# Moving tap transforms, loads and last products in a graph layer on Trainium2

## The chip, the cores and the metric

The kernel runs on one core of one Trainium2 chip. The metric is the device time of one execution in microseconds. The engines are named as the profile names them: PE (TensorE, matmuls), PEld (its weight loads), DVE (VectorE), ACT (ScalarE), POOL (GpSimd) and SP (SyncE, which here only issues transfers). DMAs are issued from the queues of SP, ACT and POOL.

## The reference, cut to what matters

x has 32 batches of 512 tokens by 256 channels, adj is 32 x 512 x 512. All is float32.

```python
h = jnp.maximum(_layernorm(x, axis=-1), 0.0)
out = x + gnn(h, adj)

def gnn(x, mask):
    xc = jnp.transpose(x, (0, 2, 1))
    c = relu(bn1(conv1d(xc, conv1_w, 0)))            # kernel size 1
    c = bn2(conv1d(c, conv2_w, 8))                   # kernel size 17
    x_conv = jnp.transpose(relu(c + xc), (0, 2, 1))
    s = x @ w_se.T + b_se                            # 3 features
    A = jnp.exp(-squared_distance(s, s)) * mask
    x_nmp = A @ relu(x @ w_msg.T + b_msg)
    gi = concat([x_conv, x_nmp]) @ w_ih.T + b_ih     # r, z, n
    gh = x @ w_hh.T + b_hh                           # r, z, n
    r = sigmoid(gi_r + gh_r); z = sigmoid(gi_z + gh_z)
    n = tanh(gi_n + r * gh_n)
    return (1.0 - z) * n + z * x
```

## The kernel before

The long convolution is done in the frequency domain. A window of 64 tokens is transformed with 80 points, so a batch has 8 windows and 16 batches make a group of 128 windows; there are two groups. The 80 rows of a spectrum are 40 units of two.

**Weights to frequencies.** The 17 taps of conv2 are loaded in eight pieces (`load_taps`, L239; tile w2p, two buffers, which the unscaled w1 of conv1 also uses once). A piece takes five DMAs, four of 16 taps and one for the seventeenth of all four quarters. `weights_to_freq` (L246) makes one step: four products `pw` with the `taps` matrix, copied out by ACT and DVE into `wst`; a piece has four steps. Each pair of steps fills an SI group of four, which four SP DMAs store to `wd` (L269). In the first step of a group DVE copies two of the four results and ACT two, in the second DVE copies one and ACT three.

**First part, once per group** (`first_part`, L779). For each batch b: `statistics` (DVE, and POOL for the power), `normalise` (DVE, tile xn), `transpose_h` (PE phT, DVE hT, store hd), `conv1` (PE pc, DVE and ACT h), `windows_to_freq` (PE px, ACT xf). The statistics run two batches ahead of conv1. In group one the 32 tap steps are spread over the batches by `between(b)`, at first two per batch, in batches 7 and 14 three; it also issues the remaining weight loads on SP. Before the first layer norm of group one, bn1's scale and shift are spread over rows by `bn1_row` (L183: ACT diagonals, PE row) and w1 is scaled by them.

**Nodes, once per group** (`nodes`, L880). Per batch: `message`, `features`, `factors`, `affinity`, `aggregate` (PE pm, psl, psr, pd, pn), and between them the products of spectra unit by unit (`product`, L367: PE py, ACT and DVE y), which `prepare` (L356) readies on POOL (wsum, both). Of group one, three units are left over; they are worked off in group two's first part by `fill()`, from the list `left`.

**Late part.** The gates of pairs of batches, with seven products where a plain 2 x 2 block scheme has eight (`gates_rz`, `gate_n`); POOL makes the operand sums. The last pair has its z gate after n (`last_z`, L637), so that the output can be blended, transposed, added to x and stored piece by piece.

**What sets the order.** Both first parts and the late part stand in `tc.manual_schedule()`: each engine runs their instructions in the order in which the code writes them. `nodes` is not in it; there the framework orders the instructions, also where its end meets the first part of group two. PSUM has eight banks of 128 x 512, handed out by `bank`.

The lines that issue the loads at the start and at group two:

```python
            load_w1()
            load_x(0)
            load_x(1)
            load_taps(gen, 0, nc.sync)
...
                combine = combine_weights()
...
                for b in range(GB, GB + 3):
                    load_x(b, nc.gpsimd)
```

Of the kernel before, what the change touches and what calls it, by code (L numbers as in the profile page):

```python
# [15 lines left out]
P = 128  # L16
# [49 lines left out]
def gnn_layer(  # L66
# [38 lines left out]
    def bank(name):  # L105
        return psum.tile([P, N], FP, tag="bank", name=name)
# [20 lines left out]
    ncol = vecs.shape[1]  # L127
    vec = consts.tile([P, ncol], FP, name="vec")
    nc.scalar.dma_start(vec, vecs)
    w1 = early.tile([P, DC, D], FP, name="w1")  # L130
    fwd = early.tile([P, 2 * L], FP, name="fwd")
    nc.scalar.dma_start(fwd, nc.inline_tensor(fwd_np, name="dft_fwd").ap())
    taps = early.tile([P, ROWS], FP, name="taps")
    nc.scalar.dma_start(taps, nc.inline_tensor(taps_np, name="dft_taps").ap())
    back = consts.tile([P, back_np.shape[1]], FP, name="back")

    GC = G // P
# [51 lines left out]
    def load_w1():  # L189

        t = W2P["w1"] = pools["gen"].tile([P, PI, D], FP, tag="w2p", name="w1_in", bufs=2)
        load_rows(t[:, :DC], w1T, nc.scalar)

    def scale_w1():
        t = W2P.pop("w1")
# [39 lines left out]
    PI = 8  # L235
    SI = 4
    W2P, WST, STATS = {}, {}, {}

    def load_taps(gen, pc, queue=nc.gpsimd):  # L239
        t = W2P[pc] = gen.tile([P, PI, D], FP, tag="w2p", name=f"w2p_{pc}", bufs=2)  # L240
        src = w2T.rearrange("(q i) k o -> q k i o", q=4)[:, :, PI * pc : PI * (pc + 1)]
        for q in range(4):
            queue.dma_start(t[32 * q : 32 * q + 16], src[q, 0:16])
        queue.dma_start(t[16::32], src[:, 16])

    def weights_to_freq(gen, pc, i):  # L246

# [389 lines left out]
    def last_z(p, terms):  # L637

        d, o, ks = RZ[p], 1, range(K3)

        def blended(src, other, i, j, t=slice(0, N)):
            z, dst = d[:, DC + i, j, t], d[:, i, j, t]
            if other is not None:
                nc.vector.tensor_add(z, other[:, t], src[:, t])
                src = z
            g = DC + i
            nc.scalar.activation(z, src, AF.Sigmoid, bias=brz[:, g : g + 1], scale=1.0)
            nc.vector.tensor_mul(dst, dst, z)
            js, half = slice(t.start // 32, t.stop // 32), slice(32 * i, 32 * (i + 1))
            if (p, j) not in OUT:  # L650
                OUT[p, j] = pools["late"].tile([P, N // 32, D // 4], FP, tag="o", name=f"o_{p}_{j}", bufs=2)
            nc.vector.transpose(OUT[p, j][:, js, half], dst.rearrange("p (j k) -> p j k", k=32))
            x = XP[p][j][:, js, half]
            nc.vector.tensor_add(x, x, OUT[p, j][:, js, half])

        b1, b2, b3, b4 = (bank(f"pz{k}_{p}") for k in range(1, 5))
        into(b1, Q1, o, ks, terms, True)
        p1 = temp("p1", f"z{p}")
        nc.scalar.copy(p1, b1)
        into(b2, Q6, o, ks, terms, True)  # L660
        u2 = temp("u2", f"z{p}")
        nc.vector.tensor_add(u2, p1, b2)
        into(b1, Q2, o, ks, terms, False)
        blended(b1, None, 0, 0)
        early_out(p, 1, 1)
        into(b2, Q7, o, ks, terms, False)
        u3 = temp("u3", f"z{p}")
        nc.vector.tensor_add(u3, p1, b2)
        early_out(p, 0, 1)
        into(b4, Q4, o, ks, terms, True)  # L670
        blended(b4, u3, 1, 0)
        store(p, 0, [nc.sync, nc.scalar])
        into(b3, Q5, o, ks, terms, True)
        blended(b3, u3, 1, 1)
        for h in range(2):
            t = slice(h * N // 2, (h + 1) * N // 2)
            into(b3, Q3, o, ks, terms, False, t)
            blended(b3, u2, 0, 1, t)
            store(p, 1, [nc.sync, nc.scalar], t)

    def gate_n(p, terms, last):
# [50 lines left out]
        closing(x3[1], 0, 1)  # L732
        for i, j in ((0, 0), (1, 1), (1, 0), (0, 1)):

            nc.vector.tensor_sub(rz[:, i, j, :], HP[p][:, 2 * i + j, :], nt[:, i, j, :])
            if last and j == 0:
                early_out(p, i, j)
            elif not last:

                blend(p, i, j, nc.gpsimd if p == B // 2 - 2 and i != j else nc.vector)  # L740


    def early_out(p, i, j):
        if (i, j) == (0, 0):
            OUT[p] = pools["work"].tile([P, N // 32, D // 4], FP, tag="x", name=f"on_{p}", bufs=3)
        OUT[p, j] = OUT[p]
        to_tokens(p, j, i)
        o = OUT.pop((p, j))
        if i != j:
            nc.vector.tensor_add(XP[p][j], XP[p][j], o)  # L750

    def blend(p, i, j, engine):
        n, d = NT[p][:, i, j, :], RZ[p][:, i, j, :]
# [25 lines left out]
    def first_part(g, freq, between, left=()):  # L779
# [6 lines left out]
        if g == 0:  # L786
            t = XN[b0] = pools["first"].tile([P, NC, D], FP, tag="xn", name="rows", bufs=2)
            ones, diags = t[:, 0, :P], t[:, 1:3, :].rearrange("p i (c m) -> p i c m", m=P)
            nc.vector.memset(ones, 1.0)
            batch_norm("bn1", scale1, shift1, nc.gpsimd)  # L790
            bn1_row(0, scale1, ones, diags)
            bn1_row(1, shift1, ones, diags)
        statistics(b0)
        normalise(b0)
        if g == 0:
# [8 lines left out]
        fill()  # L804
        statistics(b0 + 1)
        transpose_h(b0)
        normalise(b0 + 1)
        fill()
        for b in range(b0, b1):
            if b + 3 < b1:  # L810
                load_x(b + 3, nc.gpsimd)
            if b == b0:
                if g == 0:
                    for steps in between(0):
                        for step in steps:
                            step()
                conv1(b)
                fill()
            if b + 2 < b1:
# [32 lines left out]
    with tc.tile_pool(name="freq", bufs=1) as fpool:  # L852
# [3 lines left out]
        with phase("first", "gen"):  # L856
            gen = pools["gen"]
            per = N // D
            steps = [partial(weights_to_freq, gen, pc, i) for pc in range(QI // PI) for i in range(0, PI, per)]
            load_w1()  # L860
            load_x(0)
            load_x(1)
            load_taps(gen, 0, nc.sync)

            def between(b):
                if b % 2 == 0 and b // 2 + 1 < QI // PI:
                    load_taps(gen, b // 2 + 1)
                if 1 <= b <= len(load_weights):
                    load_weights[b - 1]()

                mine = spread(steps, b, GB - 1) if b < GB - 1 else [partial(load_unit, 0, u) for u in range(3)]
                return mine[:1], mine[1:]

            with tc.manual_schedule():
                xf = first_part(0, freq_tile, between)
# [41 lines left out]
        with phase("pw"):  # L917
            with phase("nodes"):
                nodes(0, xf, range(UNITS - LEFT), GB)
            with phase("first", "sums"):  # L920
                combine = combine_weights()

                def between(b):
# [4 lines left out]
                    two = [partial(sum_unit, pools["pw"], 1, b - GB + 3)] if b > GB - 3 else []  # L928
                    return combine[b - 2] if 1 < b < len(combine) + 2 else [], two

                for b in range(GB, GB + 3):
                    load_x(b, nc.gpsimd)

                pw, (u0, u1, u2) = pools["pw"], range(UNITS - LEFT, UNITS)
                left = [[partial(prepare, pw, 0, u1, xf), partial(product, pw, 0, u0, xf)],
                        [partial(prepare, pw, 0, u2, xf)],
                        [partial(product, pw, 0, u1, xf)],
                        [partial(product, pw, 0, u2, xf)]]
# [83 lines left out]
```

## Time and profile before

| | us |
|---|---|
| median of 5 runs | 1865.26 |
| lowest and highest | 1861.1, 1869.67 |
| the profiled execution | 1868.94 |
| its span, first to last instruction | 1867.2 |
| PE, DVE, ACT, POOL busy in it | 1828.3, 1115.0, 578.0, 579.1 |

A page row gives the line of the kernel, the engine, the operation, output<-inputs, shapes and count, then busy time, the mean of one, and the idle time of the engine just before with what ended it. A timeline row begins with start and length in us. A row of a window table gives the window, its length, and busy times with counts in brackets for PE, PEld, DVE, ACT and POOL, then the granted PE clock as a share of full speed, the DMA engines' busy share and GB/s.

### The profile page before, as it was taken

To read this page: it belongs to the slowest core of one execution; us is meant where nothing else is said; L and a number is where in the kernel's file an instruction comes from. 1 tells how busy PE (TensorE), PEld (TensorE's weight loads), DVE (VectorE), ACT (ScalarE), POOL (GpSimd) and SP (SyncE) were. 2 spreads that over 40 slices of the span, in tenths; PEclk is the share of its full clock that TensorE was granted. 3 is DMA by queue.
4 is the path that set the end of the run, shared out by engine and by line. 5 is a ranking of instruction groups with operands and counts; after the bars stand their busy time and mean duration, and the time that the engine had idled before them with its cause. 6 is when DMAs were issued, how large, how long until landed. Compare 5 with 4: busy or idle time off the path is not lost.

```text
span 1867.2 us, 20076 instructions
## 1 busy us (share of the span) xinstructions
PE 1828.3 (98%) x6598; PEld 1090.1 (58%) x6598; DVE 1115.0 (60%) x2238; ACT 578.0 (31%) x1075; POOL 579.1 (31%) x563
## 2 busy tenths in 40 slices
PE   7999999999899999999999999999999999999997
PEld 5777666666798666666555544555455544555443
DVE  6775655564796565555165566645665466645666
ACT  3455434332145343333222212222122221222121
POOL 3321234334332343442613322132212322133220
PEclk8999999999899999999999999999999999999999
DMA  7998988865467988767613442244422442234412
GB/s 208 301 267 234 227 238 234 226 176 187 174 224 219 222 254 239 230 190 238 179 47 72 119 118 85 38 114 119 112 69 56 118 119 87 53 97 118 118 28 41
DMA packets 306299, 289.25 MB, mean 155 GB/s; under 512 B 148028, under 2 KB 235612, under 8 KB 305812
## 3 DMA queue, kind: packets, MB, share of 16 engines
q1 hardware_dynamic: 279716, 222.64, 44.8%
q10 hardware_dynamic: 19024, 38.68, 5.9%
q0 software_dynamic: 7456, 26.65, 5.1%
q8 instruction: 53, 0.87, 0.2%
q14 instruction: 50, 0.41, 0.1%
HBM read 191.50 MB, written 96.40 MB: 154 GB/s over the span
## 4 chain that ended last, share of the span: by engine, by line
PE 89%; DMA 3%; issue 3%; DVE 2%; POOL 2%; ACT 1%; SPq 0%; ACTq 0%; POOLq 0%; DVEq 0%
PE pg L585 28%; PE pn L585 14%; PE py L385 10%; PE pn L480 10%; PE pc L320 6%; PE pm L431 5%; PE pc L573 5%; PE px L335 3%; PE pw L256 2%; PE pd L466 2%; PE phT L307 1%; DMA hT<-hd 1%; DMA sw<-ws 1%; PE psr L455 1%; PE pz L585 0%
## 5 line engine op out<-in xcount | busy, mean ns | idle before, releaser
L480 PE MATMUL pn<-A,msg 128*128 128x512 f32 x512 | 225.0, 593 | 0.0
L585 PE MATMUL pg<-hp,sw 128*128 128x512 f32 x434 | 221.8, 593 | 0.7 <-DVE rz L604 0.5
L585 PE MATMUL pg<-cp,sw 128*128 128x512 f32 x434 | 221.7, 592 | 0.3 <-DMA sw<-ws 0.3
L585 PE MATMUL pg<-np,sw 128*128 128x512 f32 x434 | 221.6, 592 | 0.0
L563 POOL TENSOR_TENSOR hp<-hp 128x512 f32<-128x512 f32 x64 | 80.4, 1266 | 412.8 <-DMA hp<-hd 351.7
L364 POOL TENSOR_TENSOR both<-xf 128x256 f32<-128x256 f32 x78 | 60.6, 777 | 333.2 <-PE py L385 299.4
L480 PEld LDWEIGHTS pn<-A,msg 128*128 128x128 f32 x512 | 97.1, 190 | 110.6 <-issue 107.7
L385 PE MATMUL py<-wt,both 128*128 128x256 f32 x624 | 150.4, 384 | 0.7 <-issue 0.7
L563 POOL TENSOR_TENSOR cp<-cp 128x512 f32<-128x512 f32 x64 | 80.4, 1268 | 225.8 <-ACT cp L579 224.5
L600 ACT ACTIVATE rz<-rz,brz 128x512 f32<-128x512 f32 x93 | 67.0, 721 | 260.2 <-DVE rz L604 260.2
L392 DVE TENSOR_TENSOR y<-y,py 128x256 f32<-128x256 f32 x78 | 31.8, 408 | 192.7 <-ACT y L391 192.7
L585 PEld LDWEIGHTS pg<-hp,sw 128*128 128x128 f32 x434 | 82.2, 190 | 104.7 <-issue 97.6
L585 PEld LDWEIGHTS pg<-cp,sw 128*128 128x128 f32 x434 | 82.4, 190 | 104.5 <-issue 103.3
L585 PEld LDWEIGHTS pg<-np,sw 128*128 128x128 f32 x434 | 82.5, 190 | 103.8 <-issue 103.8
L385 PEld LDWEIGHTS py<-wt,both 128*128 128x128 f32 x624 | 114.2, 190 | 43.3 <-issue 28.0
L472 DVE TENSOR_TENSOR A<-e,at 128x512 f32<-128x512 f32 x128 | 112.5, 916 | 36.3 <-ACT e L469 36.0
L320 PE MATMUL pc<-w,hT 128*128 128x256 f32 x512 | 124.6, 400 | 1.9 <-DVE hT L308 1.9
L351 POOL TENSOR_TENSOR wsum<-wt 128x512 f32<-128x512 f32 x78 | 107.9, 1384 | 44.5 <-DMA wt<-wd 41.4
L431 PE MATMUL pm<-wmsg,hq 128*128 128x259 f32 x512 | 117.9, 382 | 1.6 <-ACT hq L417 1.0
L704 ACT ACTIVATE nt<-nt,vech 128x512 f32<-128x512 f32 x64 | 46.2, 722 | 233.9 <-DVE nt L703 233.9
L585 PE MATMUL pn<-np,sw 128*128 128x512 f32 x224 | 114.4, 592 | 0.0
L585 PE MATMUL pn<-hp,sw 128*128 128x512 f32 x224 | 114.4, 592 | 0.0
(138 smaller groups left out, 2956.8 us busy)
## 6 DMA issues: line engine op xcount, KB each, us to landing
wt<-wd SPq DMA_DIRECT2D x160, 256.0 KB, 3.8
adj<-in_adj_dram SPq DMA_DIRECT2D x128, 256.0 KB, 5.6
wd<-wst SPq DMA_DIRECT2D x64, 320.0 KB, 5.1
yd<-y ACTq DMA_DIRECT2D x80, 256.0 KB, 3.5
yt<-yd SPq DMA_DIRECT2D x30, 640.0 KB, 7.5
hd<-hT SPq DMA_DIRECT2D x32, 512.0 KB, 4.8
nd<-nmp ACTq DMA_DIRECT2D x32, 512.0 KB, 3.7
xb<-in_x_dram SPq DMA_DIRECT2D x128, 128.0 KB, 3.7
```

Source lines behind the costliest of these rows:

```text
L320: nc.tensor.matmul(p[:, j, :], HT[b][:, ic, c * P : (c + 1) * P], w1[:, ic, :], start=(ic == 0), stop=(ic == DC - 1))
L335: nc.tensor.matmul(p[:, j * 2 * L : (j + 1) * 2 * L], H1[b][:, c0 + j, ic * P : (ic + 1) * P], fwd, start=True, stop=True)
L351: nc.gpsimd.tensor_tensor(t, WT[g, u][:, 0], WT[g, u][:, 1], op=ALU.add)
L364: nc.gpsimd.tensor_tensor(both[:, 0], re, im, op=ALU.add)
L385: nc.tensor.matmul(dst, v[:, ic, :], w[:, ic, :], start=(ic == 0), stop=(ic == DC - 1))
L431: nc.tensor.matmul(p[:, : D + NS], hq[:, ic, c * P : (c + 1) * P], wmsg[:, ic, :], start=(ic == 0), stop=(ic == DC - 1))
L472: nc.vector.tensor_mul(A[b][:, mc, :], e, at)
L480: nc.tensor.matmul(p, MSG[b][:, mc, dc * P : (dc + 1) * P], A[b][:, mc, :], start=(mc == 0), stop=(mc == NC - 1))
L563: nc.gpsimd.tensor_tensor(t[:, dst, :], t[:, a, :], t[:, b, :], op=sub)
L573: nc.tensor.matmul(bk[:, t0:t1], YT[p][j][:, c, oc * P : (oc + 1) * P], back[:, n : n + t1 - t0], start=(c == 0), stop=(c == len(spans) - ...
L585: nc.tensor.matmul(bk[:, t], sw[:, k, q, o, :], terms[k][q][:, t], start=(first and i == 0), stop=(i == len(ks) - 1), skip_group_check=True)
L600: nc.scalar.activation(rz[:, g, j, :], src, AF.Sigmoid, bias=brz[:, g : g + 1], scale=1.0)
```

## The change

Four things, of which the words name three.

- Start: the taps matrix and the first tap piece are loaded ahead of w1, x of batch 1 and fwd; the piece by SP and ACT, w1 by POOL. Of the piece's four steps, the first runs before the bn1 rows, the second between them and the statistics of batch 0, the third and fourth ahead of conv1 of batch 0. The other 28 steps go two to each of batches 1 to 14; each later piece is loaded one batch before its first step.
- Group two: its first three x are loaded by SP, ahead of the gate weights, instead of by POOL. The first left-over product follows the transposes of the group's first batch; before, it preceded them.
- Last gate: the last product of z (Q3) goes in halves to two banks of its own instead of adding to bank b3; VectorE adds b3 to u2 for it.
- Last pair: the four subtractions and one of the two additions to x run on POOL instead of DVE.

```diff
+    taps = early.tile([P, ROWS], FP, name="taps")
+    nc.scalar.dma_start(taps, nc.inline_tensor(taps_np, name="dft_taps").ap())
     w1 = early.tile([P, DC, D], FP, name="w1")
     fwd = early.tile([P, 2 * L], FP, name="fwd")
-    nc.scalar.dma_start(fwd, nc.inline_tensor(fwd_np, name="dft_fwd").ap())
-    taps = early.tile([P, ROWS], FP, name="taps")
-    nc.scalar.dma_start(taps, nc.inline_tensor(taps_np, name="dft_taps").ap())
...
-        load_rows(t[:, :DC], w1T, nc.scalar)
+        load_rows(t[:, :DC], w1T, nc.gpsimd)
...
-    def load_taps(gen, pc, queue=nc.gpsimd):
+    def load_taps(gen, pc, queues):
...
-            queue.dma_start(t[32 * q : 32 * q + 16], src[q, 0:16])
-        queue.dma_start(t[16::32], src[:, 16])
+            queues[q % len(queues)].dma_start(t[32 * q : 32 * q + 16], src[q, 0:16])
+        queues[-1].dma_start(t[16::32], src[:, 16])
...
-        b1, b2, b3, b4 = (bank(f"pz{k}_{p}") for k in range(1, 5))
+        b1, b2, b3, b4, *b5 = (bank(f"pz{k}_{p}") for k in range(1, 7))
...
         into(b3, Q5, o, ks, terms, True)
         blended(b3, u3, 1, 1)
+        nc.vector.tensor_add(u2, u2, b3)
         for h in range(2):
             t = slice(h * N // 2, (h + 1) * N // 2)
-            into(b3, Q3, o, ks, terms, False, t)
-            blended(b3, u2, 0, 1, t)
+            into(b5[h], Q3, o, ks, terms, True, t)
+            blended(b5[h], u2, 0, 1, t)
             store(p, 1, [nc.sync, nc.scalar], t)
...
-            nc.vector.tensor_sub(rz[:, i, j, :], HP[p][:, 2 * i + j, :], nt[:, i, j, :])
+            (nc.gpsimd if last else nc.vector).tensor_tensor(rz[:, i, j, :], HP[p][:, 2 * i + j, :], nt[:, i, j, :],
+                                                             op=ALU.subtract)
...
-            nc.vector.tensor_add(XP[p][j], XP[p][j], o)
+            (nc.gpsimd if j else nc.vector).tensor_tensor(XP[p][j], XP[p][j], o, op=ALU.add)
...
             batch_norm("bn1", scale1, shift1, nc.gpsimd)
+            one, two = between(0)
+            one[0]()
             bn1_row(0, scale1, ones, diags)
             bn1_row(1, shift1, ones, diags)
+            one[1]()
         statistics(b0)
         normalise(b0)
...
         statistics(b0 + 1)
         transpose_h(b0)
+        fill()
         normalise(b0 + 1)
         fill()
...
                 if g == 0:
-                    for steps in between(0):
-                        for step in steps:
-                            step()
+                    for step in two:
+                        step()
                 conv1(b)
                 fill()
...
+            load_x(0)
+            load_taps(gen, 0, [nc.sync, nc.scalar])
             load_w1()
-            load_x(0)
             load_x(1)
-            load_taps(gen, 0, nc.sync)
+            nc.scalar.dma_start(fwd, nc.inline_tensor(fwd_np, name="dft_fwd").ap())
+            first, rest = steps[: PI // per], steps[PI // per :]
 
             def between(b):
+                if b == 0:
+                    return first[:2], [partial(load_taps, gen, 1, [nc.gpsimd])] + first[2:]
                 if b % 2 == 0 and b // 2 + 1 < QI // PI:
-                    load_taps(gen, b // 2 + 1)
+                    load_taps(gen, b // 2 + 1, [nc.gpsimd])
...
-                mine = spread(steps, b, GB - 1) if b < GB - 1 else [partial(load_unit, 0, u) for u in range(3)]
+                mine = spread(rest, b - 1, GB - 2) if b < GB - 1 else [partial(load_unit, 0, u) for u in range(3)]
...
+                for b in range(GB, GB + 3):
+                    load_x(b)
                 combine = combine_weights()
...
-                for b in range(GB, GB + 3):
-                    load_x(b, nc.gpsimd)
...
-                left = [[partial(prepare, pw, 0, u1, xf), partial(product, pw, 0, u0, xf)],
+                left = [[partial(prepare, pw, 0, u1, xf)],
+                        [partial(product, pw, 0, u0, xf)],
                         [partial(prepare, pw, 0, u2, xf)],
```

## The prediction

> **What bounds the kernel now.** I read the page's share and slice rows first, then stages of the span one by one, then the timelines of the three places that the diff touches.
>
> ```profile
> span 1867.2 us, 20076 instructions
> PE   7999999999899999999999999999999999999997
> PEclk8999999999899999999999999999999999999999
> ...
> PE 89%; DMA 3%; issue 3%; DVE 2%; POOL 2%; ACT 1%; SPq 0%; ACTq 0%; POOLq 0%; DVEq 0%
> ```
>
> TensorE (PE) is full nearly everywhere; only the first, the eleventh and the last slice are not. The busy times by stage (columns: length, then PE, weight load, DVE, ACT, POOL, clock, DMA) say how much is open:
>
> ```profile
> 0.00:20.00 20.00, 10.55 (x39) 7.07 (x40) 11.18 (x38) 5.54 (x11) 7.98 (x20) 0.88 0.75 180
> 455.00:500.00 45.00, 37.98 (x140) 27.98 (x139) 25.31 (x71) 5.25 (x11) 19.29 (x22) 0.85 0.57 193
> 1780.00:1868.00 88.00, 76.13 (x186) 34.60 (x184) 59.33 (x88) 16.54 (x26) 11.31 (x8) 0.96 0.18 36
> ```
>
> PE idles 9.5 us, 7 us and 12 us there, and loses more to a half clock. The change can only win or lose in these places and in what they shift. The timeline of the start:
>
> ```profile
> 5.46 1.40 DVE L284 BATCH_NORM_STATS2 stats<-x 128x6 f32<-128x256 f32 x4 [3.71 <-DMA x<-in_x_dram]
> 9.42 1.92 PE L307 MATMUL phT<-ident,xn 128*128 128x128 f32 x8
> 13.23 3.71 PE L256 MATMUL pw<-w2p,taps 17*80 17x512 f32 x16 [1.90 <-DMA w2p<-in_w2T_dram]
> 16.88 6.21 PE L320 MATMUL pc<-w,hT 128*128 128x256 f32 x16
> ```
>
> The layer norm runs as soon as x lands, at 5.46; the two tap steps wait for their weights until 13.23, and conv1 of batch 0 starts at 16.88. The timeline around group two:
>
> ```profile
> 462.27 2.32 POOL L118 DMA_DIRECT2D x<-in_x_dram  x3
> 470.32 0.42 DVE L392 TENSOR_TENSOR y<-y,py 128x256 f32<-128x256 f32 x1 [8.58 <-ACT y L391]
> 470.65 0.42 DVE L284 BATCH_NORM_STATS2 stats<-x 128x6 f32<-128x256 f32 x1
> 474.03 3.14 DVE L296 TENSOR_SCALAR xn<-x,mv,rstd 128x256 f32<-128x256 f32 x4 [1.16 <-POOL rstd L290]
> 480.49 6.50 PE L320 MATMUL pc<-w,hT 128*128 128x256 f32 x16 [1.94 <-DVE hT L308]
> 476.00:478.00 2.00, 1.58 (x6) 1.15 (x7) 1.97 (x6) 0.00 (x0) 0.69 (x1) 0.50 0.00 0
> ```
>
> The first x of group two is issued at 462.27 and takes 8.3 us, so it lands at 470.57, just ahead of its statistics. conv1 takes 6.50 us for what is 3.46 us at full clock; the last line is a two-us stage with the clock at 0.50. The end:
>
> ```profile
> 1854.83 1.17 PE L585 MATMUL pz<-hp,sw 128*128 128x256 f32 x2 [2.41 <-DVE rz L644]
> 1858.03 0.42 DVE L644 TENSOR_TENSOR rz<-u_z,pz 128x256 f32<-128x256 f32 x1
> ```
>
> PE waits 2.41 us for VectorE to read the bank, but VectorE, when it takes the half product at 1858.03, had come straight from its previous add: it is VectorE that is late.
>
> **Start.** Removed: two SP waits. The waits of the SP queue show the present tap loads held for vec (2.2 us), fwd (1.4) and taps (2.3). Now they are five DMAs on SP and ACT right behind x and taps; w1 (four DMAs, 2.2 us of issue by the tap loads' 2.15 on that queue) goes to POOL, idle from 1.3 to 4.04; the second x, wanted at about 20, and fwd, wanted after conv1, queue behind the tap loads. Step 1's four wd stores stand before batch 0's hd store on SP, for which nobody waits. When the piece is whole: the floor is x's landing at 5.4 plus 544 KB at the 370 GB/s of that moment, 6.9; the ceiling is the third w_in DMA, at a like place in ACT's line, 9.5. I take 9.0, nearer the row.
> Added in front of the layer norm, since every engine keeps the written order: step 0 with two copies on DVE and two on ACT, the four ACT diagonals behind those copies, then step 1 and its copy on DVE, and only then the statistics. From the piece's landing: first copy after 1.1 us (13.23 to 14.32), ACT's two copies 1.1, four diagonals 1.4 and their matmuls 0.4 (4.0), step 1 1.1 to 1.9, DVE's copy 0.7: about 6.2. Statistics so start at 15.2 instead of 5.46. From there to the end of the transposes it is 5.9 us (5.46 to 11.34), so 21.1; scale_w1, the second statistics and the hT copies (0.75 + 1.9 + 1.3 behind the normalise) end at 23.5; steps 2 and 3 end between 23.3 and 24.9. conv1 starts at about 24.2 instead of 16.88: **+7.3** (+4.5 to +9).
> Given back: batch 7 loses its third step (the pw group of 16 matmuls, 2.86 us, becomes one of 8, 1.28): 1.6. Batch 14 likewise, 1.96 to 1.10: 0.9. In batches 8 to 13 the steps now fall on whole SI groups, as in 1 to 6: the second pw group averages 1.86 us there and 1.40 here: 6 x 0.46 = 2.8. At batch 14 SP issues four wd stores instead of eight (8.17 us), so the hT load at 170.19 starts up to 4 us sooner; PE idles 2.16 us between 172 and 190: I take 1.0. Against it: piece k is now needed one batch after its load. Its last DMA, issued at 63.35, took 7.6 us, to 70.95; the first step there is at 70.88. The other five spare 0.5 to 2 us; I take 0.5 in all (0 to 3). Sum -5.8, so the start is **+1.5** (-2 to +6.5).
>
> **Group two.** SP gets free at 460.4, before POOL (462.27, behind both and wsum), and x goes ahead of the 768 KB of w_hh on the same queue. The trace has x at 8.3 us with w_hh ahead of it, at 4.7 us at the kernel's start. The Trainium skill (DMA: Bandwidth & Descriptors, "Rules for kernel authors") speaks against a gain: all issuing engines feed the same 16 DMA engines, and spreading saves only issue time. By the rule alone x lands 1.8 us sooner, at 468.8; by the rows, with its new place in line, at 465.2. w_hh comes 1.4 us later, wanted only near 505; the wt load behind them waits for PE until 469.09 anyway. I take 465.2.
> What follows depends on VectorE's order, which is not written by hand here: the trace has the statistics between the two y adds of the last node product (470.32). If the statistics, through rstd, come before those adds, normalise starts behind them, at 471.2, not 474.03, though POOL's wsum and both (2.8 us) still slow it. Transposes 472.0 to 474.4; product u0, now behind them, 2.8, covers the hT copies; conv1 3.5 at full clock, ending at 480.7 instead of 487.0: **-6.3**. Bounds: -13, when normalise too precedes the adds (PE work from 469.7 to conv1 of the second batch is 17.5 us at full clock, and takes 31.5); +1, when the order stays, for then PE's gap before the transposes grows from 3.06 to 5.8 us. On that gap trace and skill differ: after gaps of 3.06 and 1.94 us the clock fell to 0.50 until 486, while the skill (TensorE: Matmul & The Clock Gate, Part 1) wants about 3.4 us idle. By the rule the 2.1 us gap left here costs nothing; by the row u0 and part of conv1 run at half clock, 3 us, and this stage brings -3.3. No single gap this short shows a fall, so I take the rule.
>
> **End.** The four subs (0.69 each) leave DVE for POOL at 1.27 each, starting as each tanh ends; the first reader comes at 1845.39, 4 us after the last sub could end: hidden by PE's products, and 1.27 per late sub if that cover is gone. The x add of 128x1024 (1.23) also goes to POOL, about 2.5 us from 1849.4, wanted by 1856.7: hidden under ScalarE's sigmoids, and late one for one beyond that. So DVE takes product Q4 0.67 us sooner. Against it the u2 add, 0.6, behind the third blend, on the path. PE's 2.41 us wait goes, but its halves were not what DVE lacked. Beside POOL, DVE's 128x1024 add took 1.53 instead of 1.23: two adds and products may grow 0.3 each. Sum **0** (-0.7 to +0.8). The banks of the gate's first products are read by 1839; no wait is added.
>
> **Sum.** +1.5 - 6.3 + 0 = -4.8 us on the profiled execution (1868.94, span 1867.2), which is 3.7 above the median of the five runs. On the median, 1865.3: **1860.5 us**.
>
> **Rivals.** (a) Slower: the layer norm behind the tap copies is not paid back. The piece lands at 9.5 or later, PE is at half clock in steps 1 to 3, conv1 starts near 26 (+9), and the slow second halves of batches 8 to 13 have a cause other than the grouping, so only the 2.5 us of the moved steps return; group two at +0.5: +7, 1872. It decides once the start's shift exceeds what comes back by more than group two wins. For it: DVE's strict order at 5 to 14 us. Against: batches 1 to 6, grouped, are 0.4 us shorter each.
> (b) The DVE order stays, and x lands for nothing: group two 0 to -1, start +1.5: 1866, no change. For it: the y add at 470.32 waits for PE, not for x.
> (c) The whole normalise passes the y adds: PE goes from product to transposes without a gap: -12, start +1: 1854. For it: DVE idles 8.58 us before 470.32. Against: in the trace nothing but statistics stands among those adds.
>
> **The numbers.** Forecast 0.34, (a) 0.28, (b) 0.17, (c) 0.21. A measurement of this kernel tells about 0.3% (5.6 us) from no change. Of the forecast 0.15 lies beyond 5.6 us faster, with nearly all of (c): 0.35. (a) mostly, with the slow edges of (b) and the forecast, is slower: 0.28. The rest, 0.37, is within. The range reaches from a somewhat smaller (c) to a somewhat larger (a): 1851 to 1874; the forecast's own is 1856 to 1865.
>
> **What would show it.** First statistics near 15 and conv1 of batch 0 near 24; the pw groups of batches 8 to 13 at 1.1 to 1.7; group two's x issued by SP near its 460.4 plus the shift, landing in under 5.5 us; statistics ahead of the last y adds; conv1 there in 3.5 us; PE without the 2.41 us wait at the end, and the last DVE steps at unchanged distances. I am wrong if the statistics still follow the y adds, if the first piece lands before 7, or if pw waits for DMA in the odd batches.

## The result, and the profile after

The kernel after takes 1874.1 us (median of 24 runs, 1870.0 to 1879.2), the kernel before 1866.3 us beside it (45 runs). The ratio is 1.0039, with a 95% interval of 1.0031 to 1.0048: 5.8 to 9.0 us slower. The prediction was 1860.5 us, 1851 to 1874, faster. The profiled execution took 1872.07 us, 2.0 below its median; that of before took 1868.94, 2.6 above its own. So these two profiles are only 3.1 us apart, and the rest of the 7.8 us does not show in them.

The page after (span; PE busy and granted clock in 40 slices; the shares of the chain that ended last):

```profile
span 1870.3 us, 20099 instructions
PE   5999999999899999999999999999999999999997
PEclk9999999999899999999999999999999999999999
...
PE 93%; issue 2%; DVE 2%; DMA 1%; POOL 1%; ACT 0%; SPq 0%; ACTq 0%; POOLq 0%; DVEq 0%
```

The first slice has fallen from 7 to 5, the eleventh is at 8 as before. The other slices say nothing new. The timeline of the start (columns: start, length, engine, line, operation, shape, count, and in brackets the idle time before it with what ended it; line numbers are one below those of before):

```profile
11.41 2.01 PE L255 MATMUL pw<-w2p,taps 17*80 17x512 f32 x8 [11.41 <-DMA w2p<-in_w2T_dram]
14.82 2.08 PE L186 MATMUL row<-rows 128*128 128x128 f32 x8 [1.41 <-ACT rows L185]
16.83 2.01 PE L255 MATMUL pw<-w2p,taps 17*80 17x512 f32 x8
...
19.59 1.39 DVE L283 BATCH_NORM_STATS2 stats<-x 128x6 f32<-128x256 f32 x4
23.16 2.20 PE L306 MATMUL phT<-ident,xn 128*128 128x128 f32 x8 [4.32 <-DVE xn L295]
25.29 4.66 PE L255 MATMUL pw<-w2p,taps 17*80 17x512 f32 x16
29.88 6.40 PE L319 MATMUL pc<-w,hT 128*128 128x256 f32 x16
```

(The four products of a step are eight instructions in the trace, so x8 is one step.) TensorE waits 11.41 us for the first tap piece, then works through step, rows, step, and waits again. The statistics start at 19.59 us and conv1 of batch 0 at 29.88, against 5.46 and 16.88; in the first 20 us TensorE is busy for 6.03 us instead of 10.55. The chain of waits names the transfer that ends the first wait, the last of the piece's DMAs that ACT issued; it took 8.53 us:

```profile
2.74 8.53 DMA w2p<-in_w2T_dram
```

Around group two:

```profile
464.96 1.55 SPq L118 DMA_DIRECT2D x<-in_x_dram  x3
...
474.72 0.42 DVE L391 TENSOR_TENSOR y<-y,py 128x256 f32<-128x256 f32 x1 [8.58 <-ACT y L390]
475.06 0.42 DVE L283 BATCH_NORM_STATS2 stats<-x 128x6 f32<-128x256 f32 x1
475.39 0.41 DVE L392 TENSOR_TENSOR y<-y,py 128x256 f32<-128x256 f32 x1
478.40 3.13 DVE L295 TENSOR_SCALAR xn<-x,mv,rstd 128x256 f32<-128x256 f32 x4 [1.13 <-POOL rstd L289]
479.90 0.45 PE L306 MATMUL phT<-ident,xn 128*128 128x128 f32 x1 [5.62 <-DVE xn L295]
...
482.71 3.47 PE L384 MATMUL py<-wt,both 128*128 128x256 f32 x8
486.88 3.62 PE L319 MATMUL pc<-w,hT 128*128 128x256 f32 x16
```

x is now issued by SP at 464.96 and takes 6.0 us, so it is there at 470.96. Its statistics start at 475.06, at once behind the y subtraction of the last node product. TensorE idles 5.62 us before the first transpose, where it had idled 3.06. The clock then is at half (row of the window table: window, length, busy times, granted clock, DMA share, GB/s), but it is product u0 and not conv1 that runs in it:

```profile
482.00:484.00 2.00, 2.00 (x9) 1.73 (x8) 1.97 (x10) 0.00 (x0) 0.59 (x1) 0.50 0.00 0
```

The end, VectorE's side:

```profile
1836.66 1.64 DVE L699 TENSOR_TENSOR nt<-nt,p_n 128x512 f32<-128x512 f32 x1
...
1856.23 0.68 DVE L643 TENSOR_TENSOR rz<-u_z,pz 128x512 f32<-128x512 f32 x1
1859.61 0.69 DVE L653 TENSOR_TENSOR xb<-xb,o 128x512 f32<-128x512 f32 x1
1860.22 0.68 DVE L674 TENSOR_TENSOR u_z<-u_z,pz 128x512 f32<-128x512 f32 x1
1861.01 0.42 DVE L643 TENSOR_TENSOR rz<-u_z,pz 128x256 f32<-128x256 f32 x1
...
1865.85 0.42 DVE L653 TENSOR_TENSOR xb<-xb,o 128x256 f32<-128x256 f32 x1
```

The add to u2 (1860.22) stands between the third blend's last add and the first half's add. An add beside GpSimd's subtraction takes 1.64 us instead of 0.69.

Put side by side, the lag of after behind before, at the same piece of work in the two profiled executions:

| start of | before | after | lag, us |
|---|---|---|---|
| conv1, batch 0 | 16.88 | 29.88 | 13.0 |
| conv1, batch 2 | 39.56 | 52.74 | 13.2 |
| conv1, batch 15 | 165.25 | 173.41 | 8.2 |
| last aggregate of group one | 460.26 | 464.66 | 4.4 |
| end of conv1, batch 16 | 486.99 | 490.50 | 3.5 |
| first add of the last gate (u_z) | 1843.69 | 1846.04 | 2.4 |
| end of the span | 1867.2 | 1870.3 | 3.1 |

Three parts are to be explained: 13 us lost in the first 30 us, 5 us won back until batch 15, and next to nothing from group two and the end. The fall from 8.2 to 4.4 is a fourth; the last section shows that stretch to differ as much between executions of code that is the same there.

### The profile page after: what moved, and what is told of

The parts are those of the page before. It is cut to its first block, busy times and chain, and to the rows that moved or that the text cites. A ratio compares the mean times of both kernels' runs of the same rounds, so it can differ in the third digit from the quotient of the medians.

```text
span 1870.3 us, 20099 instructions
## 1 busy us (share of the span) xinstructions
PE 1822.1 (97%) x6598; PEld 1086.1 (58%) x6598; DVE 1110.9 (59%) x2234; ACT 578.5 (31%) x1075; POOL 586.1 (31%) x569
## 4 chain that ended last, share of the span: by engine, by line
PE 93%; issue 2%; DVE 2%; DMA 1%; POOL 1%; ACT 0%; SPq 0%; ACTq 0%; POOLq 0%; DVEq 0%
PE pg L584 29%; PE pn L584 14%; PE pn L479 11%; PE py L384 11%; PE pm L430 6%; PE pc L319 6%; PE pc L572 5%; PE px L334 3%; PE pw L255 2%; PE pd L465 2%; PE phT L306 1%; DMA w2p<-in_w2T_dram 1%; PE psr L454 1%; PE pz L584 1%; DVE stats L283 0%
## 5 line engine op out<-in xcount | busy, mean ns | idle before, releaser
L584 PE MATMUL pn<-cp,sw 128*128 128x512 f32 x224 | 114.4, 592 | 0.0
```

The lines of the kernel that those rows point to most:

```text
L584: nc.tensor.matmul(bk[:, t], sw[:, k, q, o, :], terms[k][q][:, t], start=(first and i == 0), stop=(i == len(ks) - 1), skip_group_check=True)
```

## The experiments

Twelve kernels were run, each timed beside the kernel before on the same chip. The ratio is to before, with its 95% interval; before had a median of 1865.7, 1866.2 and 1866.5 us in the three groups of four.

| kernel | median, us | ratio |
|---|---|---|
| start_only | 1871.4 | 1.0037 (1.0022 to 1.0052) |
| group2_only | 1866.2 | 1.0006 (0.9992 to 1.0020) |
| tail_only | 1865.8 | 1.0000 (0.9990 to 1.0009) |
| norm_first | 1865.6 | 0.9997 (0.9987 to 1.0007) |
| start_gap | 1858.6 | 0.9955 (0.9939 to 0.9972) |
| start_gap_w1_last | 1865.8 | 0.9998 (0.9986 to 1.0009) |
| g2_defer | 1859.6 | 0.9967 (0.9951 to 0.9982) |
| tail_pipe | 1864.9 | 0.9997 (0.9987 to 1.0007) |
| early_only | 1865.7 | 0.9993 (0.9983 to 1.0003) |
| tail_pipe2 | 1861.8 | 0.9978 (0.9969 to 0.9987) |
| best1 | 1849.8 | 0.9907 (0.9883 to 0.9931) |
| best2 | 1852.1 | 0.9921 (0.9902 to 0.9940) |

**One part at a time.** start_only has the hunks of the start, the loads, the places of the first piece's steps and the spreading of the rest:

```diff
+            load_taps(gen, 0, [nc.sync, nc.scalar])
...
+            one[0]()
             bn1_row(0, scale1, ones, diags)
             bn1_row(1, shift1, ones, diags)
+            one[1]()
```

> The kernel before with the start's edits alone (loads, the first piece's steps beside the layer norm, two steps per batch after it). Theory 1, each part costs what its stage shows in the two profiles: conv1 of batch 0 begins near 29.9 us instead of 16.9, conv1 of batch 15 about 8 us later than before's 165.3, and the time is 1872 to 1875, the whole of the loss. Theory 2, the medians are 7.8 us apart but the two profiled executions only 3.1, because the start's loss is mostly won back in the node stage (there the lag falls from 8.2 to 4.4) and the rest of the loss lies in later parts: then this kernel is at 1869 to 1871. Forecast of before the result: 1868.

The start alone costs as much as the whole change within what the measurement can tell: 4.1 to 9.7 us against 5.8 to 9.0. Its profile has conv1 of batch 0 at 29.93 and of batch 15 at 173.00, as after has. Its median is a little under theory 1's range, and a part of theory 2's 1869 to 1871 lies inside the interval too. So this time alone does not part the two; what decides is that the other parts cost nothing that can be measured.

group2_only has the loads of x and the split list:

```diff
-                left = [[partial(prepare, pw, 0, u1, xf), partial(product, pw, 0, u0, xf)],
+                left = [[partial(prepare, pw, 0, u1, xf)],
+                        [partial(product, pw, 0, u0, xf)],
```

> The kernel before with x of group two on SP and the split list of left-over steps alone. Theory 1: VectorE takes the statistics behind the same y subtraction as before (near 470.6), TensorE waits over 5 us for the transposes instead of 3.06, product u0 and not conv1 runs at half clock, conv1 ends 0.9 us sooner: 1865 to 1866. Theory 2 (w_hh and what follows on SP is late and costs in the batches after): 1868 to 1871. The forecast had 1860.

No difference. From the start of the last aggregate to the end of conv1 of batch 16 it takes 25.8 us in this profile, 25.8 in after's, 26.7 in before's. But the eight profiles that have this stage as in before show 25.4 to 26.7, so not even a gain of 0.9 us in the stage is shown.

tail_only has the edits to the last gate and the last pair:

```diff
+        nc.vector.tensor_add(u2, u2, b3)
...
+            into(b5[h], Q3, o, ks, terms, True, t)
+            blended(b5[h], u2, 0, 1, t)
```

> The kernel before with the last gate's banks of its own, its u2 add, and the subtractions and one add on GpSimd alone. Theory 1: the u2 add stands whole on the path, 0.7 to 0.9 us, the rest cancels (VectorE's 128x512 add takes 1.64 us beside GpSimd's instead of 0.69, twice): 1867.0 to 1867.5, and the last 30 us are longer by 0.9. Theory 2 (TensorE's 2.41 us wait was on the path): 1864 to 1865.

No difference in time. From u_z to the end of the span it is 24.1 us in its profile, 24.3 in after's, 23.5 in before's: 0.6 to 0.8 us longer, about the length of the u2 add (0.68). But the seven profiles whose end is as in before show 23.5 to 24.3, so a cost of the add is not shown.

**Where the start loses.** norm_first is the kernel after with one thing undone: all four steps stand where before has its two.

```diff
-            one[0]()
             bn1_row(0, scale1, ones, diags)
             bn1_row(1, shift1, ones, diags)
-            one[1]()
...
-                    for step in two:
+                    for step in two[:1] + one + two[1:]:
```

> The kernel after, but all four steps of the first piece stand where before has its two, behind the layer norm and in front of conv1 of batch 0; the early loads and all else stay. Theory 1 (the place of the steps is what costs): statistics at 5.5 us again, conv1 of batch 0 between 18 and 21 us instead of 29.9, the time 9 to 11 us under after's: 1863 to 1866. Theory 3 (the new order of the loads is what costs: x of batch 1 lands at 12.8, w1 near 10, and VectorE waits for them in front of the hT and tap copies): conv1 of batch 0 at 23 or later and the time 1868 or more.

```profile
5.38 1.41 DVE L283 BATCH_NORM_STATS2 stats<-x 128x6 f32<-128x256 f32 x4 [3.63 <-DMA x<-in_x_dram]
12.26 10.13 PE L255 MATMUL pw<-w2p,taps 17*80 17x512 f32 x32 [0.51 <-DMA w2p<-in_w2T_dram]
22.32 5.84 PE L319 MATMUL pc<-w,hT 128*128 128x256 f32 x16
```

The statistics are back at 5.38 us, and the time is 8.5 us under after's. The place of the steps is what costs: of the 13.0 us by which conv1 of batch 0 was late, 7.6 are gone. The other 5.4 stay, and conv1 starts at 22.32, later than theory 1 had it, since the four steps in one stretch take 10.13 us where before's two take 3.71; the time still is theory 1's. Theory 3 does not hold: the piece is there at 12.26, sooner than in before (13.23), and conv1 starts before 23.

start_gap puts the steps where TensorE idles anyway: two as in before, two behind the transposes of batch 1.

```diff
                 if g == 0:
-                    for step in two:
+                    for step in two[:1] + one:
                         step()
                 conv1(b)
...
             if b == b0:
+                if g == 0:
+                    for step in two[1:]:
+                        step()
                 fill()
```

> The kernel before with the start's early loads and two steps per batch, but steps 0 and 1 of the first piece behind the layer norm, as in the kernel before, and steps 2 and 3 behind the transposes of batch 1, where the kernel before has TensorE idle from 24.0 to 27.4 us. If the loss of the start is the place of the four steps and the gain of the grouping is real (batches 7 to 14 gave back 4.9 us of 13.0 between conv1 of batch 2 and of batch 15 in the profile after): conv1 of batch 0 near 17, of batch 1 near 29 as before, of batch 15 about 4 us sooner than before's 165.3, the time 1861 to 1863. If the early loads cost something themselves (x of batch 1 and w1 later), conv1 of batch 0 is at 19 or later and the time 1865 or more. If the grouping's gain is no gain of the whole: 1866.

```profile
23.15 1.04 PE L306 MATMUL phT<-ident,xn 128*128 128x128 f32 x8
24.12 3.45 PE L255 MATMUL pw<-w2p,taps 17*80 17x512 f32 x16
27.51 2.33 PE L306 MATMUL phT<-ident,xn 128*128 128x128 f32 x8
```

The 16 products of steps 2 and 3 (3.45 us) fill the stretch in which before waits 3.42 us for the normalise, and the transposes behind them start at 27.51 where before starts them at 27.38. conv1 of batch 15 starts at 160.09, 5.2 us sooner than before's. The time is 7.6 us under before's (5.2 to 11.4 by the interval), better than expected. Two steps more than in before are done by conv1 of batch 2, and it starts only 0.3 us later (39.90 against 39.56).

early_only splits that gain: the new order of loads, with the steps placed and spread as in before.

```diff
-                    for step in two[:1] + one:
-                        step()
+                    for some in between(0):
+                        for step in some:
+                            step()
...
-                mine = spread(rest, b - 1, GB - 2) if b < GB - 1 else [...]
+                mine = spread(steps, b, GB - 1) if b < GB - 1 else [...]
```

> The kernel before with the start's new order of loads alone; its steps stay as they were, two in front of conv1 of batch 0 and then two or three per batch. It splits start_gap's 7.6 us. If the gain is the grouping (two whole steps per batch): conv1 of batch 0 at 17 to 18, conv1 of batch 2 to batch 15 in 125.5 us as before (start_gap 120.2), the time 1865 to 1867. If the early loads bring it: 1860 to 1862.

Nothing that can be measured comes from the loads (0.9993). From conv1 of batch 2 to that of batch 15 it takes 125.5 us here and 125.7 in before. With two whole steps per batch it takes 120.2 to 121.4 in all seven kernels that have it, whatever their start looks like: after 120.7, start_only 121.4, norm_first 121.1, start_gap 120.2, start_gap_w1_last 120.5, best1 121.1, best2 120.3. So the spreading, and not the loads, is worth about 5 us there. It is two things. In before, batches 2 to 14 do 28 steps, in these seven kernels 26: without their third steps, batches 7 and 14 take 1.0 and 0.9 us less in the profile after (from conv1 to the next conv1, 12.45 to 11.45 us and 8.84 to 7.99). Batches 8 to 13, whose two steps now make up a whole SI group, take 3.0 us less together. The two moved steps are a gain only where they cost nothing at the start, as in start_gap.

start_gap_w1_last asks why the piece landed so late.

```diff
-        load_rows(t[:, :DC], w1T, nc.gpsimd)
+        load_rows(t[:, :DC], w1T, nc.scalar)
```

(The scaling of w1 is moved behind the two steps as well.)

> As start_gap, but w1 goes behind the taps on ACT's queue instead of beside them on GpSimd's, and is scaled behind the two steps. It asks why the first piece landed at 11.3 us instead of my 9.0. If w1's 256 KB in the same stretch are the cause (the DMA engines are full from 4 to 13 us in the profile after, at 144 to 271 GB/s), the piece lands 1.5 to 2 us sooner than in start_gap. If the tap DMAs into 16 partitions are slow by themselves, it lands within 0.5 us of start_gap's. The time within 2 us of start_gap's either way, for conv1 waits for w1 next.

The four tap DMAs took 7.5 us (SP) and 8.0 us (ACT) in the median, with w1 beside them 7.2 and 8.1. Issuing w1 5 us later did not shorten them, so w1 is not the cause of their length; what is, stays open between the tap transfers' shape and the other 512 KB loads. The second half of the expectation was wrong: ACT's queue issues w1 from 6.87 to 11.23 us, the row diagonals stand behind that on ACT, and conv1 of batch 0 starts at 21.55 instead of 17.42; the time is 7 us above start_gap's.

**Group two.** g2_defer moves the last node product of group one behind the statistics and the normalise in the written order.

```diff
                 for u in mine[2:]:
-                    product(pools["pw"], g, u, xf)
+                    if g == 0 and i == GB - 1:
+                        prepare(pools["pw"], g, u, xf)
+                    else:
+                        product(pools["pw"], g, u, xf)
...
-                left = [[partial(prepare, pw, 0, u1, xf)],
+                left = [[partial(product, pw, 0, u0 - 1, xf), partial(load_unit, 0, u2), partial(prepare, pw, 0, u1, xf)],
                         [partial(product, pw, 0, u0, xf)],
```

> The kernel before with x of group two on SP, the split list, and the last node product of group one moved behind the statistics and the normalise of group two's first batch in the written order (its load and sums stay). If the early x brought nothing because VectorE takes the statistics behind that product's y subtraction (475.06 in the profile after, 4.1 us after x's landing): statistics start at about 466.8, the transposes at 471, TensorE's gap falls from 5.6 to about 1 us, u0 and conv1 run at full clock, conv1 ends 7 us sooner than before's 487.0: 1859 to 1861. If GpSimd's rstd, behind wsum and both, or the DMA of x is the next bound: a gap of 3 us stays and the time is 1863 to 1866.

```profile
458.12 1.56 SPq L118 DMA_DIRECT2D x<-in_x_dram  x3
463.00 1.41 DVE L284 BATCH_NORM_STATS2 stats<-x 128x6 f32<-128x256 f32 x4 [3.70 <-DMA x<-in_x_dram]
464.69 1.89 PE L385 MATMUL py<-wt,both 128*128 128x256 f32 x8
466.02 1.38 DVE L296 TENSOR_SCALAR xn<-x,mv,rstd 128x256 f32<-128x256 f32 x4 [1.13 <-POOL rstd L290]
467.28 1.04 PE L307 MATMUL phT<-ident,xn 128*128 128x128 f32 x8
471.30 3.79 PE L320 MATMUL pc<-w,hT 128*128 128x256 f32 x16 [0.39 <-DVE hT L308]
```

Now the statistics follow x and not the product: x is issued at 458.12 and they start at 463.00. The product (464.69) covers statistics and normalise, the transposes follow it with no idle time, and conv1 takes 3.79 us. From the last aggregate to the end of conv1 it is 17.3 us, 9.5 less than in before. The time is 6.7 us lower (3.4 to 9.1). In after and group2_only the same early x brought nothing that can be told; the order on VectorE held its gain back. The new order with the late x was not run. In before x lands 10.3 us after the last aggregate starts, here the statistics start 5.2 us after it, so an estimate from these is that about 5 of the 9.5 us need the early x.

**The end.** tail_pipe keeps the edits of the tail and writes three adds ahead.

```diff
-        blended(b3, u3, 1, 1)
+        summed(b3, u3, 1, 1)
         nc.vector.tensor_add(u2, u2, b3)
-        for h in range(2):
-            t = slice(h * N // 2, (h + 1) * N // 2)
+        halves_t = [slice(h * N // 2, (h + 1) * N // 2) for h in range(2)]
+        for h, t in enumerate(halves_t):
             into(b5[h], Q3, o, ks, terms, True, t)
-            blended(b5[h], u2, 0, 1, t)
-            store(p, 1, [nc.sync, nc.scalar], t)
+            summed(b5[h], u2, 0, 1, t)
+        blended(None, None, 1, 1)
+        for t in halves_t:
+            blended(None, None, 0, 1, t)
+            store(p, 1, [nc.sync, nc.scalar], t)
```

> The kernel before with the tail's edits, and the adds of the last three blends written ahead of the third blend's sigmoid, so that VectorE does the u2 add and both half adds in the 1.2 us that it waits for ScalarE there, and the last sigmoids run beside VectorE's other work. If VectorE and its turns with ScalarE set the end (and not TensorE, whose last product ends 9 us before the span in the profile after): the end comes 2.5 to 3.5 us sooner than in tail_only, 1862.5 to 1864. If TensorE or the store behind the last add sets it: 1865.5 to 1866.5.

Not in the time (0.9997). From u_z to the end of the span it is 22.5 us, 1.0 less than before (and below all seven profiles with before's end) and 1.6 less than tail_only, half of what was expected:

```profile
1863.50 0.88 ACTq L780 DMA_DIRECT2D out_dram<-xb  x2
1864.43 0.51 ACT L650 ACTIVATE rz<-rz,brz 128x256 f32<-128x256 f32 x1 [4.20 <-DVE xb L657]
1864.97 0.42 DVE L651 TENSOR_TENSOR rz<-rz 128x256 f32<-128x256 f32 x1 [1.54 <-ACT rz L650]
```

ACT issues the first half's store (ACTq, 0.88 us) in front of the last sigmoid, and VectorE waits 1.54 us for it. tail_pipe2 moves the sigmoids ahead of the store, into `summed`:

```diff
-            src = src if src is not None and other is None else z
-            g = DC + i
-            nc.scalar.activation(z, src, AF.Sigmoid, bias=brz[:, g : g + 1], scale=1.0)
+            if src is not None:
+                summed(src, other, i, j, t)
```

> As tail_pipe, but the last two sigmoids are written ahead of the first half's store, whose issue (0.88 us on ACT's queue) stood in front of the last sigmoid there (1864.43, VectorE idle 1.54 us). Expected: the end 1.5 us sooner than in tail_pipe, 2.2 us sooner than before's from the last gate's first add; the time 1863 to 1865. If the store is what the end waits for: no change against tail_pipe.

```profile
1846.31 1.65 ACT L646 ACTIVATE rz<-rz,brz 128x512 f32<-128x512 f32 x3 [3.66 <-DVE rz L644]
1850.83 2.13 ACTq L781 DMA_DIRECT2D out_dram<-xb  x4
...
1851.60 0.42 DVE L658 TENSOR_TENSOR xb<-xb,o 128x256 f32<-128x256 f32 x1
```

All three sigmoids run in one stretch at 1846.31, and VectorE works without a pause to its last add. From u_z to the end it is 21.3 us, 2.2 less than in before, as expected, and 2.2 to 3.0 less than in the seven profiles with before's end. The time is 4.8 us lower (2.4 to 5.8); the low end of the interval meets these figures, and for anything beyond them the profiles show no cause.

**Together.** best1 is start_gap, g2_defer and tail_pipe2 in one. best2 differs from it by one thing:

```diff
+        if g == 0:
+            transpose_h(b0)
         statistics(b0 + 1)
-        transpose_h(b0)
+        if g > 0:
+            transpose_h(b0)
```

> start_gap, g2_defer and tail_pipe2 in one kernel. If the three parts add (-7.6, -6.7 and about -2): 1849 to 1852. If one takes from another (all act through TensorE's idle stretches in different stages, so this is not expected): 1854 or more.

> As best1, with the hT copies of batch 0 ahead of the statistics of batch 1 on VectorE. In start_gap VectorE waits for x of batch 1 until 12.96 us, and hT and TensorE's second step behind it (1.47 us idle). Expected: that gap goes, conv1 of batch 0 1 to 1.5 us sooner; the time 0 to 1.5 us below best1.

best1 is 16.8 us faster than before (12.9 to 21.8), and 24 us faster than after. The sum of the parts (7.6, 6.7 and 4.8) is 19.1, within the interval. best2 is no better, against what was expected: 1852.1, conv1 of batch 0 at 16.77 against best1's 16.48. Group two even fell short in best1's profile:

```profile
457.51 1.41 DVE L283 BATCH_NORM_STATS2 stats<-x 128x6 f32<-128x256 f32 x4 [5.95 <-DMA x<-in_x_dram]
460.47 1.26 POOL L350 TENSOR_TENSOR wsum<-wt 128x512 f32<-128x512 f32 x1
460.53 3.13 DVE L295 TENSOR_SCALAR xn<-x,mv,rstd 128x256 f32<-128x256 f32 x4 [1.13 <-POOL rstd L289]
462.03 0.30 PE L306 MATMUL phT<-ident,xn 128*128 128x128 f32 x1 [2.33 <-DVE xn L295]
```

x took 7.1 us to land here, 4.9 in g2_defer. So the normalise came 2.2 us later against the same aggregate, met GpSimd's sums, and took 3.13 us instead of 1.38. From the last aggregate to the end of conv1 it is 21.8 us here, against 17.3. So g2_defer's gain in this stage hangs on x landing in time.

## Why the prediction was wrong

The likeliest case failed in two of its three parts. The outcome is its rival (a), by that rival's first half: the layer norm behind the tap copies is not paid back. That rival's +7 us lies near the 7.8 between the medians by luck: it had too small a shift (+9, measured +13.0) and too little given back (2.5, measured 5.0).

- **The piece's landing** was put at 9.0 us, with 9.5 as the ceiling. It was 11.3 (+2.4 on the first product, at 11.41). The ceiling came from the third w_in DMA in the profile before, a transfer of other shape with other neighbours; the floor came from a rate of 370 GB/s that the 512 KB x transfers had. In the profile after, the DMA engines are fully busy from 4 to 12 us while moving 144 to 204 GB/s up to 10.
- **From the landing to the statistics** 6.2 us were counted; it took 8.2. Every product there ran at half rate: each of the two steps took 2.01 us, counted at 1.1 and at 1.1 to 1.9, and the row products ended 1.26 us behind the last diagonal, counted at 0.4. The steps' cost was taken from 13.23 us on in before, where TensorE had already worked; here the step is the first thing that it does. Before's own first products, the rows, show what such a start costs, 2.07 us for eight:

```profile
7.56 2.07 PE L187 MATMUL row<-rows 128*128 128x128 f32 x8 [7.56 <-ACT rows L186]
```

  The profile's clock column does not show it in after:

```profile
11.40:13.40 2.00, 1.99 (x8) 0.36 (x8) 0.00 (x0) 0.00 (x0) 0.00 (x0) 1.00 1.09 339
```

  Eight products in 1.99 us are at half the rate of later ones (1.10 us for the same eight), in a window whose clock reads 1.00: the clock record has no entry before its first rise, which in this profile is at 35.3 us. The Trainium skill (TensorE: Matmul & The Clock Gate, Part 1) has the half rate as the state from which the array starts, until some 3.4 us of work; the prediction used that part for gaps and forgot the start. The start at half rate agrees with the trace, the 3.4 us do not: TensorE had done 18.2 us of products by 35.3. The last section says which.
- **From the statistics to the end of the transposes** 5.9 us were counted; 5.8 (19.59 to 25.36). This held.
- **From there to conv1** 3.1 us were counted; 4.5. Steps 2 and 3 took 4.66 us, at half rate and behind copies.
- So the shift of conv1 was +7.3 by the sum, +13.0 in the trace, past its upper bound of 9. The terms miss by 2.4, 2.0, -0.1 and 1.4.
- **Given back** until batch 15 were 4.8 (1.6, 0.9 and 2.8, less 0.5 for pieces that land just in time): measured 5.0 (1.0, 0.9 and 3.0, and 0.1 in batches 2 to 6), and in six other kernels 4.3 to 5.5. This step was right, mechanism and size, as was the small price of the pieces: one product group waits 0.28 us for its piece in the profile after. It speaks against the rival's second assumption, that the grouping was not the cause of the slow second halves. The 1.0 us counted for the hT load behind batch 14 cannot be told in the stretch that follows.
- **Group two** was put at -6.3, and came to -0.9 in the two profiles, which is within the spread of unchanged code. The failing step is that the statistics would pass the y adds. They stayed where they were, 4.1 us behind x's landing (470.96; put at 465.2 in the frame of before, 466.6 there by the trace). This is rival (b)'s outcome for this stage, and the prediction had its price: a gap of 5.8 us before the transposes (measured 5.62), 0 to -1 in all. g2_defer showed that the mechanism itself was right: with the order forced, the stage gives 9.5 us. The order there is made by the framework, so it could not be read from the change, and yet the forecast and rival (c), 0.55 of the chance together, rested on it.
- **The clock** in the same step: the gap of 2.1 us did not come about in after, so this did not decide the outcome. But the reason for taking the rule, that no single gap this short shows a fall, was a misreading of the profile before. There a single gap of 1.43 us is followed by half the clock, from 496.4 to 499.8:

```profile
494.47 1.71 PE L307 MATMUL phT<-ident,xn 128*128 128x128 f32 x8 [1.43 <-DVE xn L296]
496.00:498.00 2.00, 2.00 (x8) 1.65 (x7) 1.97 (x11) 0.00 (x0) 0.00 (x0) 0.60 0.92 230
```

  best1 later had nearly the gap in question, 2.33 us in front of the transposes (462.03, above), and the clock was at 0.50 from 463.0 to 466.4.
- **The end** was put at 0, up to +0.8. By the profiles it is +0.6 to +0.8, which agrees with the u2 add and lies within the spread of unchanged code as well. TensorE's 2.41 us wait vanished and brought nothing that can be measured, as was said.

In place of +1.5 - 6.3 + 0, the stages of the two profiles give +8.2, -0.9 and +0.8, or 8.1, beside 7.8 between the medians. Only the first of them is larger than what single executions differ by. What lies between (the fall of the lag from 8.2 to 4.4 in the nodes of group one, and another 1.1 us later) did not come up in the medians: start_only, which shows the same fall, is as slow as after. Most of the 3.8 us is before's single execution, as the last section shows; whether the new start has a small part in it stays open.

## What to carry to other kernels

Work that starts on the first engine to be ready is not free when another engine's first task is written behind it: on engines that keep the written order, put early work into a stretch in which that engine waits, not ahead of the chain that the start depends on. An earlier transfer pays only if the instruction that reads it is first in line on its engine; look for what stands ahead of the reader, and move that. Cost the first products of a kernel at the rate that an idle TensorE starts with, and a transfer's landing by transfers of its own shape. Before a stage's change is read from two profiles, look how far the stage differs between profiles of code that is the same there.

## What was not expected

**The clock falls after short gaps, and also without one.** In group2_only, in the nodes of group one:

```profile
226.87 1.57 PE L466 MATMUL pd<-sr,sl 9*128 9x512 f32 x4 [0.30 <-DVE y L392]
228.37 3.63 PE L385 MATMUL py<-wt,both 128*128 128x256 f32 x8
229.00:230.00 1.00, 1.00 (x4) 0.80 (x3) 0.25 (x4) 1.00 (x3) 0.00 (x0) 0.50 1.06 223
```

TensorE idles 0.30 us, and the granted clock is at 0.50 from about 228.6 to 232. In tail_pipe a gap of 1.99 us at the same place is followed by over 6 us at 0.50. These gaps, and the 1.43 and 2.33 us above, are shorter than the 3.4 us of idleness that the Trainium skill (TensorE: Matmul & The Clock Gate, Part 1) gives.

The products around the gap of 0.30 us use nine rows of the array (9*128), and two other profiles speak for the rows as a cause. In start_gap the two tap steps (17 rows, 3.45 us) fill the gap at 24.12; TensorE is busy for 6.51 of 6.60 us, and the clock falls all the same:

```profile
22.00:28.60 6.60, 6.51 (x35) 3.15 (x33) 5.20 (x18) 3.77 (x7) 1.79 (x2) 1.00 0.94 253
28.80:32.00 3.20, 3.20 (x11) 2.76 (x10) 3.17 (x12) 0.00 (x0) 0.00 (x0) 0.50 0.89 255
```

In norm_first the four tap steps run at half rate through all of their 10.13 us (1.06 us for a product in the median, 0.59 in start_gap), and the clock rises only at 26.6, 4.3 us into conv1, whose products use 128 rows. So products with few rows seem not to raise the clock, nor to hold it; that would also explain why the start of after stays at half rate up to 35.3, 5.4 us into its conv1. It is argued from these traces: no run changed the rows alone.

**Stages have a spread of their own.** From conv1 of batch 15 to the last aggregate of group one it takes 295.0 us in before, 296.1 in group2_only, 298.5 in tail_pipe, and 291.1 to 292.5 in the other four profiles with before's start, none of which changes anything up to there but a few loads; 290.8 to 291.3 in the seven with two whole steps per batch. A pair of profiles can differ by 7 us there for no edit at all, as much as the whole effect under study. From the end of conv1 of batch 16 to the last gate it is 1354.6 to 1359.6 us in the fourteen profiles, in no order that follows the edits.

**VectorE slows beside GpSimd.** A 128x512 add takes 1.64 us instead of 0.69 beside GpSimd's subtraction, and the normalise of four tiles 3.13 instead of 1.38 beside its sums. In the profile after, that add starts at 1836.66, while GpSimd's subtraction runs until 1837.74, and ends 0.56 us behind it. This fits the exclusive lock on the port pair that the two engines share, as the Trainium skill (SBUF — State Buffer, SBUF: two separate sides) has it: the later one waits for the whole instruction of the other. Work handed to GpSimd is paid for in part by VectorE.
